# Masking and storing the sorted attention weights block by block in steps 3 to 6 of a recurrent scan, and loading the sorted rows of steps 8 to 11 in step 4

## The chip, the cores and the metric

The kernel runs on one core of one Trainium2 chip, in one launch. The metric is the device time in microseconds (us) of a run; of the kernel before there are three such runs, and one more execution that was profiled. Everything below that carries a start time is taken from that profiled execution, counted from the start of its span.

## What is computed

A batch of 1024 users, each with a history of 100 item embeddings of 128 numbers, goes through two recurrent scans. Cut to what matters here:

```python
keys = GRU(history)                                  # [1024, 100, 128]
score = MLP(concat(keys, q, keys - q, q * keys))     # q: the item in question
attn = softmax(where(mask == 1, score, -inf))        # over the 100 steps
pooled = einsum('bt,btd->bd', attn, keys)            # [1024, 128]
att_seq = pooled.T[:100]        # column t of pooled is the weight of step t
def augru_step(h, (x_t, a_t)):                       # x_t = keys[:, t]
    r = sigmoid([h, x_t] @ Wr.T + br)
    u = sigmoid([h, x_t] @ Wu.T + bu)
    h_hat = tanh([h * r, x_t] @ Wh.T + bh)
    u = a_t[:, None] * u
    return (1 - u) * h + u * h_hat
attention_feature = state of the step sequential_length - 1
scores = MLP(concat(user, item, hist_sum, item * hist_sum, attention_feature))
```

The update weight `a_t` of the second scan (AUGRU) is a column of `pooled`: it is known only when the whole first scan, the softmax and the pooled sum are done.

## The kernel before, in words

The batch lies along the free dimension: a tile is 128 hidden units by 512 users, and there are two halves (`i` = 0 and 1). The first part, `gru_phase`, runs the 100 steps of the GRU with the attention scores, the running softmax and the pooled sum beside them. It ends at about 1400 us of the span.

The second part, `augru_phase`, runs steps 1 to 99 of AUGRU on users sorted by length, so that a column is dropped when its user's history is over. Three versions of it are in the program (for three shapes of the list of lengths), and a branch picks one; the one that ran here starts with 384 columns per half and has 44 at the end. The constants give for it: `one` = 88, `cover[99]` = columns 340 to 384, and `LAST * PR` = 320.

Steps 1 to 87 run as half steps, `half_step(t, i)`, each with six matrix products of 384 columns at first. In one half step TensorE (PE) does: the product of the half before with `r` (`ph`, line 1425), the products with this half's state (`pr`, `pu`, line 1425), and the three products with the keys of the half after (`open_gates`, line 1421). VectorE (DVE) does, in this order: `pu*c` of the half before (1465), `r = h*pr` (1467), the new state of the half before (1469), `pu*att` (1470), `rest` (1473), and the transposition of the keys of step t+2 (`load_key`, 1403). ScalarE (ACT) does three activations. The two halves alternate, so PE fills the time in which one half waits for its activations. Steps 88 to 99 do both halves at once (`whole_step`); there a single chain through PE, ACT and DVE sets the pace.

What surrounds the change:

- **The weights.** `store_pooled` (1296) writes `pooled` to HBM in 8 stores. `gather_weights` (indirect DMAs by POOL, line 195) reads the users back in sorted order, four gathers for each half, into `att_r`. `mask_weights` (1358) zeroes the weights behind each user's end, in one DVE operation over the steps 4 to 99. `store_weights` turns the result in four blocks of 32 steps (transpositions, 1364) and stores each to `late_d` (1368); `load_att` (1387) then reads the row of one step back, spread over 128 partitions, into `at`. The rows of step 4 are read behind the first block's store, those of step t+2 in step t from step 3 on. Steps 1 to 3 have their weights from another, earlier path (`att_d`).
- **The queues.** All these stores and loads but the gathers are issued by SyncE (SP), in program order; a load that waits for a store to land holds whatever SP issues behind it.
- **The sorted rows.** The keys of steps 0 to 11 lie in HBM sorted by user (`sorted_d`). Those of steps 8 to 11 are loaded by `load_sorted` (242) into two tiles of the pool `kp3`; the first transposition from them is `load_key(8, i)` in step 6. The keys of step 12 on come by row gathers (POOL, 249), each behind a one-column copy (248) that paces it by `rest`.
- **The predictor.** The last MLP runs for groups of 128 users when their columns are over. For three groups it is a generator, `predict_held`, that `whole_step` advances three times in a step: `turn()` between the openings of `pr`/`pu` and the closing of `ph`, `turn()` between the opening of `ph` and the products with `rest`, and once at the end of the step. The row product is `rows` (1638); for the second and third group the last product of the group before (1637) stands ahead of it.

Of the kernel before, what the change touches and what calls it, by code (L numbers as in the profile page):

```python
# [19 lines left out]
P = 128  # L20
B = 1024
T = 100
# [29 lines left out]
G = 4  # L52
# [61 lines left out]
def kernel(ctx: ExitStack, tc: tile.TileContext, a: dict, out: bass.AP):  # L114
# [123 lines left out]

    def load_sorted(q, i, tile):

        rows[q, i] = tile
        nc.sync.dma_start(out=tile[:, :, : G * R], in_=sorted_d[i][ts(q, P)])

# [1056 lines left out]
    def augru_phase(pools, alive, delay):  # L1300
# [17 lines left out]
        ]  # L1318
        one = apart[-1] + 1
        ends = group_ends(alive, delay)  # L1320
# [34 lines left out]

        def mask_weights(i):
            later_rows = sorted_rows[i][:, :, SOON:T]
            nc.vector.tensor_mul(later_rows, later_rows, used_s[:, i])

        def store_weights(i):  # L1360

            turned = wp.tile([P, P // R, GH * R], F32, tag="att_t", name="att_t", bufs=2)
            for b in range(P // R):
                nc.vector.transpose(
                    turned[:, b, :].rearrange("p (g r) -> p g r", r=R),
                    sorted_rows[i][:, :, ts(b, R)],
                )
                nc.sync.dma_start(
                    out=late_d[i][ts(b, R), :].rearrange("c (p s) -> p c s", s=P),
                    in_=turned[:, b, :],  # L1370
                )
                if b == 0:
                    load_att(SOON, i)

        def load_att(t, i):
# [60 lines left out]
        def half_step(t, i):  # L1436
# [40 lines left out]
            resets[t, i] = r, pu, rest  # L1477
            if (t, i) in ((2, 1), (3, 0)):
                mask_weights(t % 2)
            if (t, i) == (1, 0):  # L1480
# [3 lines left out]
            elif after[0] == one < T:  # L1484
                open_both(one, "pr", "pu", "ph")
            if (t, i) == (2, 1):
                store_weights(0)
            elif (t, i) == (3, 0):
                store_weights(1)
            if SOON - 2 < t < T - 2:  # L1490
# [102 lines left out]
        def predict_held(groups):  # L1593
# [19 lines left out]

            def state_of(g):
                state = sp.tile([P, NH, PR], F32, name="state3")
                nc.scalar.copy(state, h_all[:, :, ts(g, PR)])
                return state
# [15 lines left out]
            for k, g in enumerate(groups):  # L1633
                p = tile_of("rows")
                p2 = p[:, HB - 1 :]
                if k:
                    nc.tensor.matmul(p2, lhsT=f1, rhs=later["m2"], start=True, stop=True)
                nc.tensor.matmul(
                    p[:, :M0],
# [4 lines left out]
                )  # L1644
                yield
                yield
# [216 lines left out]
        sorted_rows = [gather_weights(i) for i in range(NH)]  # L1863
        for half in later["halves"]:
            load_sorted(2, half.i, kp.tile([P, KH, 2 * G * R], F32, tag="rows", name="rows"))
        ahead, due = iter(()), []
# [10 lines left out]
        for t in range(1, T):  # L1877
# [6 lines left out]
            for i in range(NH):  # L1884
                if t < one:
                    half_step(t, i)
                elif i == 0:
                    whole_step(t, lambda: next(held, None))
                for _ in range(due.pop(0) if due else 0):
                    next(ahead, None)  # L1890

                if t < one:
                    take_turn(2 * G)
                elif i == 0:
                    next(held, None)
# [10 lines left out]
            if t == HALF_TIME:  # L1906
                last_places()
                for m, to in zip((wr, wu), minus):
                    nc.gpsimd.tensor_scalar_mul(to, m[:, 0, :], -1.0)
                nc.gpsimd.tensor_scalar_mul(later["m0_minus"], later["m0"][:, 4, :], -1.0)  # L1910
        all_of(held)
        for _, job in jobs:
            all_of(job)
        earlier_results()
        if one == T:
            open_state(T - 1, 1)
            next(final)
            last_state(1)
        all_of(final)
# [102 lines left out]
```

## Time and profile before

| | us |
|---|---|
| median of 3 runs | 1978.48 (1976.69 to 1979.32) |
| the profiled execution's own time | 1971.09 |
| its span | 1968.9 |
| PE busy | 1957.7 of the span |
| DVE, ACT, POOL busy | 1637.3, 935.1, 1256.5 |
| bytes moved by DMA | 220.17 MB |

A row of the timeline gives the start, the length, the engine, the line, the operation with output and inputs, how many instructions are merged in the row, and in brackets the idle time before it with what ended it. Starts of consecutive rows of one line tell the pace: they can be closer than the lengths, since an engine starts one instruction while the last results of the one before are still coming out. Rows of SP are the issuing of a DMA and not its transfer.

### The profile page before, as it was taken

Reading aid. Unit: us, or ns where it says so; the run is one execution under the profiler, and the core shown is the slowest. Engines: PE = TensorE matmul, PEld = TensorE weight load, DVE = VectorE, ACT = ScalarE, POOL = GpSimd, SP = SyncE. Lnnn points to the kernel's source line nnn. Section 1 sums busy time; section 2 is a strip of 40 time slices with the busy share of each in tenths; the row PEclk is TensorE's granted clock in tenths of the full one; section 3 lists DMA queues with packets and bytes.
Section 4 is the critical chain, followed back from the end, with each engine's and each line's share of the span. In section 5 each row is a group of like instructions: output and inputs, shape, how many; then the busy total and the mean of one; then the engine's idle time right before and its main releaser. Section 6 shows DMA issues by size and latency. Waiting matters only on the chain.

```text
span 1968.9 us, 40928 instructions
## 1 busy us (share of the span) xinstructions
PE 1957.7 (99%) x15270; PEld 846.7 (43%) x15270; DVE 1637.3 (83%) x2976; ACT 935.1 (47%) x1676; POOL 1256.5 (64%) x1348
## 2 busy tenths in 40 slices
PE   9999999999999999999999999999999999999998
PEld 3333333333333333333333333333555556789898
DVE  7888888888888888888878888888787788888896
ACT  4444454454545454454545444455444444455554
POOL 1324859678696969688695949798754444454432
PEclk9999999999999999999999999999999999999999
DMA  4453333233333443347743333323543333335441
GB/s 117 110 110 103 109 100 102 77 99 117 107 112 116 102 119 102 91 139 218 208 157 109 99 104 108 94 81 122 156 140 103 98 98 94 103 93 120 115 81 40
DMA packets 257173, 220.17 MB, mean 112 GB/s; under 512 B 53871, under 2 KB 219348, under 8 KB 256196
## 3 DMA queue, kind: packets, MB, share of 16 engines
q1 hardware_dynamic: 245476, 185.15, 33.7%
q0 software_dynamic: 11200, 32.04, 5.6%
q8 instruction: 122, 2.00, 0.4%
q14 instruction: 87, 0.71, 0.1%
q10 hardware_dynamic: 288, 0.26, 0.0%
HBM read 154.90 MB, written 60.85 MB: 110 GB/s over the span
## 4 chain that ended last, share of the span: by engine, by line
PE 97%; POOL 1%; DMA 1%; DVE 0%; SPq 0%; issue 0%; ACT 0%; another core or an unknown queue 0%; POOLq 0%; DVEq 0%; ACTq 0%
PE ps L665 52%; PE pm L851 17%; PE ph L1425 4%; PE pu L1425 4%; PE pr L1425 4%; PE pu L1421 4%; PE ph L1421 4%; PE pr L1421 4%; POOL pooled L777 1%; POOL kw L776 1%; PE pr L1516 0%; DMA x<-in_hist_x 0%; DMA att_r<-pooled_d,idx_w 0%; PE pu L1516 0%; PE ph L1516 0%
## 5 line engine op out<-in xcount | busy, mean ns | idle before, releaser
L665 PE MATMUL ps<-x,wih 128*32 128x512 f32 (+1 forms) x4808 | 588.1, 591 | 1.7 <-DMA x<-in_hist_x 1.4
L665 PE MATMUL ps<-hn,whh 128*32 128x512 f32 x4752 | 582.7, 592 | 0.0
L677 ACT ACTIVATE r<-ps,brz 128x512 f32<-128x512 f32 x200 | 137.8, 689 | 446.2 <-PE ps L665 443.4
L665 PEld LDWEIGHTS ps<-x,wih 128*32 128x32 f32 x4808 | 157.6, 110 | 359.5 <-issue 319.6
L665 PEld LDWEIGHTS ps<-hn,whh 128*32 128x32 f32 x4752 | 155.7, 110 | 354.1 <-issue 350.8
L649 POOL TENSOR_TENSOR xm<-x,m 128x512 f32<-128x512 f32 x200 | 234.3, 1172 | 74.3 <-DMA m<-mask_d 73.7
L650 POOL TENSOR_TENSOR hist<-hist,xm 128x512 f32<-128x512 f32 x200 | 258.8, 1294 | 15.7
L777 POOL TENSOR_TENSOR pooled<-pooled,kw 128x512 f32<-128x512 f32 (+1 forms) x195 | 250.2, 1283 | 15.3
L776 POOL TENSOR_TENSOR kw<-kt,e 128x512 f32<-128x512 f32 (+1 forms) x195 | 210.0, 1077 | 70.4 <-DVE e L1009 70.4
L249 POOL DMA_INDIRECT rows<-keys_d,idx_k x186 | 180.4, 970 | 75.8 <-POOL rows L248 69.3
L685 DVE SCALAR_TENSOR_TENSOR u<-ps,bhh,r 128x512 f32<-128x512 f32 x198 | 147.8, 747 | 91.3 <-PE ps L665 88.4
L698 ACT ACTIVATE ps<-ps,bih 128x512 f32<-128x512 f32 x198 | 131.1, 662 | 189.0 <-DVE ps L695 189.0
L1433 ACT ACTIVATE c<-ph,bh 128x384 f32<-128x384 f32 (+38 forms) x174 | 88.2, 507 | 257.0 <-PE ph L1425 256.9
L851 PE MATMUL pm<-hn,wk 128*32 128x512 f32 x1188 | 205.8, 592 | 0.0
L851 PE MATMUL pm<-kq,wkq 128*32 128x512 f32 x1188 | 205.7, 592 | 0.0
L851 PE MATMUL pm<-mv,w 128*32 128x512 f32 x790 | 187.6, 592 | 0.0
L708 DVE TENSOR_TENSOR d<-hn,ps 128x512 f32<-128x512 f32 x198 | 136.1, 688 | 36.0 <-ACT ps L698 35.9
L248 POOL COPY rows<-rest 128x1 f32<-128x1 f32 x186 | 35.4, 190 | 196.8 <-DVE rest L1473 176.2
L709 DVE TENSOR_TENSOR d<-ps,d 128x512 f32<-128x512 f32 x198 | 137.0, 692 | 26.4 <-ACT ps L699 14.3
L695 DVE TENSOR_TENSOR ps<-ps,u 128x512 f32<-128x512 f32 x200 | 139.9, 700 | 22.6 <-PE ps L665 1.9
L710 DVE TENSOR_TENSOR ps<-ps,d 128x512 f32<-128x512 f32 x198 | 138.4, 699 | 6.7
L730 DVE STREAM_TRANSPOSE kt<-hn 128x512 f32<-128x512 f32 x200 | 140.3, 701 | 3.3 <-ACT hn L717 3.3
(342 smaller groups left out, 3000.3 us busy)
## 6 DMA issues: line engine op xcount, KB each, us to landing
x<-in_hist_x SPq DMA_DIRECT2D x211, 256.0 KB
keys_d<-kt SPq DMA_DIRECT2D x44, 1024.0 KB
m<-mask_d SPq DMA_DIRECT2D x200, 128.0 KB
at<-late_d SPq DMA_DIRECT2D x46, 192.0 KB
wide_d<-kt SPq DMA_DIRECT2D x24, 256.0 KB
sorted_d<-sort SPq DMA_DIRECT2D x32, 192.0 KB
rows<-sorted_d SPq DMA_DIRECT2D x6, 1024.0 KB
s_b<-mv SPq DMA_DIRECT2D x200, 8.0 KB
```

Of the source, the lines that this page charges most:

```text
L249: nc.gpsimd.indirect_dma_start(out=r[:, k, :], out_offset=None, in_=keys_d[q], in_offset=bass.IndirectOffsetOnAxis(ap=idx_k[:, k, i : i + ...
L649: nc.gpsimd.tensor_mul(d, x, m)
L650: nc.gpsimd.tensor_add(acc, acc, d)
L665: nc.tensor.matmul(p[ts(q, R), cs], lhsT=w[:, g, ts(q, R)], rhs=v[:, cs], start=(j == 0), stop=(j == len(parts) - 1),)
L685: nc.vector.scalar_tensor_tensor(out=u, in0=ph, scalar=bhh[:, 2:3], in1=r, op0=ALU.add, op1=ALU.mult,)
L695: nc.vector.tensor_add(pi, pi, u)
L730: nc.vector.transpose(kt[:, :, n, :], h.rearrange("p (k r) -> p k r", r=R))
L776: eng.tensor_mul(d, k, w)
L777: eng.tensor_add(acc, acc, d)
L851: nc.tensor.matmul(p[i][s, :], lhsT=w[:, s], rhs=v, start=start, stop=stop)
L1421: nc.tensor.matmul(p, lhsT=m[:, 1, :], rhs=v, start=True, stop=False)
L1425: nc.tensor.matmul(p, lhsT=m[:, 0, :], rhs=v, start=False, stop=True)
```

## The change

The one DVE operation that masked a half's weights is cut into four, one for each block of 32 steps, and `store_weights` becomes a generator: a half step of the steps 3 to 6 takes one block, masks it, turns it, stores it, and (first block) loads the row of step 4. Before, half 0 was masked, turned and stored whole in half step (2, 1), and half 1 in (3, 0). The load of the sorted rows of steps 8 to 11 moves from the start of AUGRU to behind the half steps of step 4, and takes the 12 blocks of users that are in use instead of 16. In `predict_held` one `yield` moves up, so that the row product comes a turn later. The new formula for `one` gives 88 again for the version that ran; the branch at the end of `augru_phase` is for `one == T`, which that version does not reach; the assertion makes no instruction.

```diff
-    def load_sorted(q, i, tile):
+    def load_sorted(q, i, tile, n=KH):
         rows[q, i] = tile
-        nc.sync.dma_start(out=tile[:, :, : G * R], in_=sorted_d[i][ts(q, P)])
+        nc.sync.dma_start(out=tile[:, :n, : G * R], in_=sorted_d[i][ts(q, P), :n])
...
-        one = apart[-1] + 1
+        one = T if cover[T - 1][0] < LAST * PR else apart[-1] + 1
...
-        def mask_weights(i):
-            later_rows = sorted_rows[i][:, :, SOON:T]
-            nc.vector.tensor_mul(later_rows, later_rows, used_s[:, i])
-
         def store_weights(i):
             turned = wp.tile([P, P // R, GH * R], F32, tag="att_t", name="att_t", bufs=2)
             for b in range(P // R):
+                steps = slice(max(SOON, b * R), min(T, (b + 1) * R))
+                later_rows = sorted_rows[i][:, :, steps]
+                nc.vector.tensor_mul(
+                    later_rows,
+                    later_rows,
+                    used_s[:, i, :, steps.start - SOON : steps.stop - SOON],
+                )
                 nc.vector.transpose(
...
                 if b == 0:
                     load_att(SOON, i)
+                yield
...
-            if (t, i) in ((2, 1), (3, 0)):
-                mask_weights(t % 2)
             if (t, i) == (1, 0):
                 open_gates(1, 1, ("pr", "pu"))
...
-            if (t, i) == (2, 1):
-                store_weights(0)
-            elif (t, i) == (3, 0):
-                store_weights(1)
+            if t == G - 1:
+                stores.append(store_weights(i))
+            if t >= G - 1 and stores:
+                next(stores[i], None)
             if SOON - 2 < t < T - 2:
                 load_att(t + 2, i)
...
                 if k:
                     nc.tensor.matmul(p2, lhsT=f1, rhs=later["m2"], start=True, stop=True)
+                yield
                 nc.tensor.matmul(
                     p[:, :M0],
...
-                yield
                 yield
                 if k:
                     result(groups[k - 1], p2)
...
-        for half in later["halves"]:
-            load_sorted(2, half.i, kp.tile([P, KH, 2 * G * R], F32, tag="rows", name="rows"))
+        stores = []
+        third = [kp.tile([P, KH, 2 * G * R], F32, tag="rows", name="rows") for _ in range(NH)]
...
                     half_step(t, i)
+                    if t == G:
+                        load_sorted(2, i, third[i], blocks[FIRST[2]].stop)
```

On DVE, from the last `rest` of half step (2, 1) on, the program before reads (numbers behind a name tell buffers apart; `att_r` are the gathered weights, `att_t` the turned ones, `k` the keys, `c` the tanh):

```order
L1473 SCALAR_TENSOR_TENSOR rest<-pu,h_all 128x384
L1358 TENSOR_TENSOR att_r<-att_r,used_s 128x4x96
L1364 STREAM_TRANSPOSE att_t<-att_r 128x128 x4
L1403 STREAM_TRANSPOSE k_14904<-rows 128x384
L1465 TENSOR_TENSOR pu<-pu,c_14907 128x384
L1467 TENSOR_TENSOR r_14914<-h_all,pr 128x384
L1469 TENSOR_TENSOR h_all<-pu,rest 128x384
L1470 TENSOR_TENSOR pu<-pu,at 128x384
```

Half step (3, 0) begins at `pu<-pu,c`. In the same place the changed program has on DVE:

```order
L1477 SCALAR_TENSOR_TENSOR rest<-pu,h_all 128x384
L1407 STREAM_TRANSPOSE k_14890<-rows 128x384
L1469 TENSOR_TENSOR pu<-pu,c_14893 128x384
L1471 TENSOR_TENSOR r_14900<-h_all,pr 128x384
L1473 TENSOR_TENSOR h_all<-pu,rest 128x384
L1474 TENSOR_TENSOR pu<-pu,at 128x384
L1477 SCALAR_TENSOR_TENSOR rest<-pu,h_all 128x384
L1362 TENSOR_TENSOR att_r<-att_r,used_s 128x4x28
L1367 STREAM_TRANSPOSE att_t<-att_r 128x128
```

The mask of half 0 now stands one half step (six DVE operations) later, and one block of it at a time. On SP, the program before issues at the start of AUGRU (`late_d_82` is that of half 0, `late_d_83` of half 1):

```order
L1296 DMA pooled_d<-pooled 32x16x32 x8
L242 DMA rows<-sorted_d_72 128x16x128
L242 DMA rows<-sorted_d_73 128x16x128
L1368 DMA late_d_82<-att_t 4x32x128
L1387 DMA at<-late_d_82 128x384
L1368 DMA late_d_82<-att_t 4x32x128 x3
L1368 DMA late_d_83<-att_t 4x32x128
L1387 DMA at<-late_d_83 128x384
L1368 DMA late_d_83<-att_t 4x32x128 x3
```

The changed program issues there, on SP:

```order
L1296 DMA pooled_d<-pooled 32x16x32 x8
L1371 DMA late_d_82<-att_t 4x32x128
L1391 DMA at<-late_d_82 128x384 x2
L1371 DMA late_d_83<-att_t 4x32x128
L1391 DMA at<-late_d_83 128x384 x2
L1371 DMA late_d_82<-att_t 4x32x128
L1391 DMA at<-late_d_82 128x384
L242 DMA rows<-sorted_d_72 128x12x128
L1371 DMA late_d_83<-att_t 4x32x128
L1391 DMA at<-late_d_83 128x384
L242 DMA rows<-sorted_d_73 128x12x128
```

The loads of the sorted rows went behind the first store of each half and its loads; the second load of `at` behind each first store is that of step 5. On PE, the third group's row product in the whole steps of the program before (`m_9352` are the weights of the attention feature):

```order
L1506 MATMUL pu<-k_19765,wu 128x88
L1637 MATMUL rows<-m_9646,f_19785 128x1
L1638 MATMUL rows<-m_9352,state_19787 128x200
L1516 MATMUL ph<-r_19803,wh 128x88
L1506 MATMUL ph<-k_19765,wh 128x88
L1516 MATMUL pr<-rest,minus_14754 128x88
```

and in the changed program on PE:

```order
L1508 MATMUL pu<-k_19771,wu 128x88
L1640 MATMUL rows<-m_9646,f_19791 128x1
L1518 MATMUL ph<-r_19808,wh 128x88
L1508 MATMUL ph<-k_19771,wh 128x88
L1642 MATMUL rows<-m_9352,state_19793 128x200
L1518 MATMUL pr<-rest,minus_14754 128x88
```

The product of 200 columns moved from ahead of the closing of `ph` to behind its opening.

More of the change, by code (lines that the diff above doesn't have):

```diff
@@ L1614, in state_of @@
             def state_of(g):
+                assert ends[g] < t
                 state = sp.tile([P, NH, PR], F32, name="state3")
@@ L1910, in augru_phase @@
                 nc.gpsimd.tensor_scalar_mul(later["m0_minus"], later["m0"][:, 4, :], -1.0)
+        if one == T:
+            open_state(T - 1, 1)
+            last_state(1)
         all_of(held)
@@ L1914, in augru_phase @@
         earlier_results()
[L1915 to L1918, printed above, removed]
         all_of(final)
```

## The prediction

> **What bounds the kernel now.** I read the page first, for the engine that sets the end, then PE's and DVE's waits, then the timeline where the longest of them falls.
>
> ```profile
> span 1968.9 us, 40928 instructions
> PE 1957.7 (99%) x15270; PEld 846.7 (43%) x15270; DVE 1637.3 (83%) x2976; ACT 935.1 (47%) x1676; POOL 1256.5 (64%) x1348
> PE ph L1425 <- DVE r L1467: 2.9, 2, 2.8
> DVE att_r L1358 <- DMA att_r<-pooled_d,idx_w: 3.6, 1, 3.6
> ```
>
> PE is busy 99% of the span, so only what PE loses can be won: 1968.9 - 1957.7 = 11.2 us are not busy, and the change adds and removes no matrix product. Its one long wait is 2.8 us for `r` from DVE, and DVE's one wait of that size is 3.6 us for the gathered weights, ahead of the mask. PE's closings of `ph` show the place:
>
> ```profile
> 1418.10 0.81 PE L1425 MATMUL ph<-r,wh 128*128 128x384 f32 x2
> 1424.88 0.91 PE L1425 MATMUL ph<-r,wh 128*128 128x384 f32 x2 [2.75 <-DVE r L1467]
> 1429.17 0.91 PE L1425 MATMUL ph<-r,wh 128*128 128x384 f32 x2 [0.15 <-DVE r L1467]
> 1433.15 0.81 PE L1425 MATMUL ph<-r,wh 128*128 128x384 f32 x2
> 1437.02 0.81 PE L1425 MATMUL ph<-r,wh 128*128 128x384 f32 x2
> ```
>
> The last two are one half step apart: 3.87 us. Three half steps lie between 1418.10 and 1433.15, which is 15.05 us where 3 x 3.87 = 11.61 would do. PE loses **3.44 us** here, more than the idle times of 2.75 and 0.15, because the second and third closings come late too. DVE over the same stretch:
>
> ```profile
> 1415.69 0.57 DVE L1465 TENSOR_TENSOR pu<-pu,c 128x384 f32<-128x384 f32 x1 [0.78 <-ACT c L1433]
> 1416.31 0.55 DVE L1467 TENSOR_TENSOR r<-h_all,pr 128x384 f32<-128x384 f32 x1
> 1417.25 0.56 DVE L1470 TENSOR_TENSOR pu<-pu,s_b 128x384 f32<-128x384 f32 x1
> 1417.84 0.56 DVE L1473 SCALAR_TENSOR_TENSOR rest<-pu,h_all 128x384 f32<-128x384 f32 x1
> 1421.98 0.56 DVE L1358 TENSOR_TENSOR att_r<-att_r,used_s 128x384 f32<-128x384 f32 x1 [3.59 <-DMA att_r<-pooled_d,idx_w]
> 1422.58 0.89 DVE L1364 STREAM_TRANSPOSE att_t<-att_r 128x128 f32<-128x128 f32 x4
> 1432.44 0.56 DVE L1470 TENSOR_TENSOR pu<-pu,at 128x384 f32<-128x384 f32 x1
> 1435.23 0.56 DVE L1467 TENSOR_TENSOR r<-h_all,pr 128x384 f32<-128x384 f32 x1
> 1438.48 0.57 DVE L1465 TENSOR_TENSOR pu<-pu,c 128x384 f32<-128x384 f32 x1 [0.61 <-ACT c L1433]
> 1938.53 0.30 DVE L1565 TENSOR_TENSOR pu<-pu,at 128x128 f32<-128x128 f32 x1
> ```
>
> Behind the mask at 1421.98 stand in DVE's queue the four turns and half step (3, 0) with its `r`, which PE waits for. Two margins matter for later. In a settled half step DVE idles 0.61 us (1438.48). And `r` is done at 1435.23 + 0.56 = 1435.79, while PE takes it at 1437.02: **1.23 us** by which DVE may be late before PE loses anything.
>
> **Part 1: the mask moves one half step on.** I put the half steps on PE's undisturbed pace. `r` of (2, 1) at 1416.31 served the closing at 1418.10. Then `r` comes at 1420.18 for (3, 0), 1424.05 for (3, 1), 1427.92 for (4, 0), 1431.79 for (4, 1). `rest` begins 1.53 us after `r` (1417.84 - 1416.31) and is over some 0.5 later, so DVE reaches the first mask of half 0 at about 1422.2 and that of half 1 at about 1426.1. When are the weights there?
>
> ```profile
> 1417.03 0.94 POOL L195 DMA_INDIRECT att_r<-pooled_d,idx_w  x1 [0.31 <-issue]
> 1422.03 1.33 POOL L195 DMA_INDIRECT att_r<-pooled_d,idx_w  x1 [0.30 <-issue]
> DMA to landing us min/median/max: 3.7/5.2/5.9
> 1411.54 2.63 SPq L242 DMA_DIRECT2D rows<-sorted_d  x2
> 1415.00:1420.00 5.00, 5.00 (x17) 2.92 (x16) 2.62 (x5) 2.62 (x5) 3.78 (x5) 1.00 0.94 343
> 1420.00:1425.00 5.00, 2.25 (x8) 1.07 (x7) 2.98 (x9) 0.76 (x2) 2.75 (x3) 1.00 0.22 66
> ```
>
> These are the last gather of each half, the time from issue to landing of all eight, the issue of the two sorted loads, and two windows (last columns: granted clock, DMA share, GB/s). The last gather of half 0 landed by 1421.98, 4.95 us after its issue; the mask at 1422.2 finds it there. The last gather of half 1 is issued at 1422.03 in either kernel, since POOL's issuing of eight in a row sets that; with 4.95 it lands at 1427.0, 0.9 us behind DVE. So the wait of 3.59 goes, and 0.9 us of waiting (none with 3.7, 1.8 with 5.9) may come one half step later, which the 1.23 us of margin cover, but for the longest landing. Nothing in it costs PE by itself, so this part is worth **-3.44 us**. The two sorted loads also leave the time of the gathers: 1415 to 1420 is when the rings were 0.94 busy. That can only shorten the landings; I count nothing for it, for the issuing of half 1's last gather does not move.
>
> **Part 2: the cut mask.** One operation of 384 elements becomes three of about 128 and one of 16 per half, a block each half step from (3, 0) to (6, 1). A DVE product of 128 elements takes 0.30 us (1938.53), a turn 0.89 / 4 = 0.22. That is 0.52 us more per half step against 0.61 of idle: nothing on PE's path, and were the idle time gone, at most 8 x 0.52 = 4.2 us against the 1.23 of margin; but it stands there in the row. The Trainium skill's page "VectorE: DVE Perf Modes", section "The DRAIN you can't avoid", speaks against cutting an operation: the next one does not start until the pipe is empty, so one should minimize the count. By that, the six operations of a half step would fill six times their length, 6 x 0.56 = 3.36, and mask and turn 0.57 more, together 3.93 us and 0.06 more than PE's 3.87; over six half steps 0.4 us, still inside the margin. The trace has starts closer than lengths: from `r` at 1435.23 to the idle time that ends at 1438.48, five operations pass in 3.25 - 0.61 = 2.64 us, 0.53 each for a length of 0.56. So I keep the 0.52.
>
> **Part 3: the rows of step 4 come back later, relative to their use.** This is what is late next. Before, store and load had slack, because PE had lost 3.44 us; now the store is issued at the same moment and its user is earlier.
>
> ```profile
> 1422.91 0.57 SPq L1368 DMA_DIRECT2D late_d<-att_t  x1
> 1425.52 0.34 SPq L1387 DMA_DIRECT2D at<-late_d  x1
> 1425.95 2.40 SPq L1368 DMA_DIRECT2D late_d<-att_t  x4
> 1431.79 0.34 SPq L1387 DMA_DIRECT2D at<-late_d  x1
> ```
>
> Half 0: mask and turn from 1422.2 to about 1422.8, store, and the load 2.61 us later as here (1425.52 - 1422.91), at 1425.4. How long a load of `at` takes to land, no row says. It is no less than the store's 2.61 (three times the bytes), and no more than the 4.4 us that the second one had: its user stands one half step behind 1432.44, at 1436.2, and shows no wait. So it lands between 1428.0 and 1429.8. (4, 0) needs it 0.94 us after its `r` (1417.25 - 1416.31), at 1428.9: 0 to 0.9 us of waiting, inside the margin of 1.23. Half 1: masked when its gather has landed, 1427.0, stored at 1427.6. In the row of four stores the fourth is half 1's first, issued about 1427.8, and the load that waits for it went out at 1431.79, 4.0 us later, among other transfers. With 2.6 to 4.0 the load goes out at 1430.2 to 1431.6 and lands at 1432.8 to 1436.0. Its user is due at 1431.79 + 0.94 = 1432.7, and PE loses from 1432.7 + 1.23 = 1434.0 on. The middle of the landings, 1434.4, costs 0.4 us; the ends cost nothing and 2.0. I take **+0.2**, toward the low end, since fewer stores are under way than in that row. What SP holds meanwhile: behind the waiting load stand the `at` of step 5, due a whole step later, and the second block's store, whose steps 32 on nobody reads before step 30. The DMA page of the Trainium skill, "DMA: Bandwidth & Descriptors", section "Anatomy of one DMA", gives 2.0 us plus the bytes over 436 GB/s; by it an estimate for the load (196,608 bytes) is 2.45 us, and with that for both loads this part would cost 0 and the time be 0.2 lower. The store of 65,536 bytes would be 2.15 us by the same rule, and the row has 2.61.
>
> **Part 4: the sorted rows of steps 8 to 11.** 12 of 16 blocks: 786,432 bytes a half. They go out after the second block's store, about 1431 to 1433 for half 0 and 1435 to 1437 for half 1. `load_key(8, 0)` stands 2.7 us behind `pu*c` of (6, 0): 1419.56 + 6 x 3.87 + 2.7 = 1445.5, and half 1's at 1449.3. Two such loads of 1 MB ran in the window of 343 GB/s; at that rate one takes 2.3 us, and even doubled, with 2 us of latency, half 1 is in at about 1444. Nothing, unless the rate collapses (rival below). The row gathers of POOL start some 3 us earlier than before and share the rings; they are due in step 10.
>
> **Part 5: the predictor's row product.** In the whole steps PE, ACT and DVE wait for each other in turn, so the place of a product counts.
>
> ```profile
> 1948.05 0.25 DVE L1564 TENSOR_TENSOR r<-h_all,pr 128x88 f32<-128x88 f32 x1 [0.45 <-ACT pr L1553]
> 1948.36 0.58 PE L1638 MATMUL rows<-m,state 128*128 128x200 f32 x2
> 1948.78 0.35 PE L1516 MATMUL ph<-r,wh 128*128 128x88 f32 x2
> 1949.41 0.39 PE L1516 MATMUL pu<-rest,minus 128*128 128x88 f32 x2
> 1949.84 0.46 PE L1516 MATMUL pr<-c,wr 128*128 128x88 f32 x2
> 1950.67 0.25 DVE L1564 TENSOR_TENSOR r<-h_all,pr 128x88 f32<-128x88 f32 x1 [0.30 <-ACT pr L1553]
> 1950.97 0.46 PE L1516 MATMUL ph<-r,wh 128*128 128x88 f32 x2
> ```
>
> Without the product `ph` begins 0.30 us behind the start of `r` (1950.97 - 1950.67); with it 0.73. So its 0.42 us (1948.78 - 1948.36) lie on the chain. Behind the opening of `ph` they fall where PE has room: the last product with `rest` is done at about 1949.63 and `pr<-c` starts at 1949.84, 0.2 us of the 0.42. I expect 0.42 won and 0.22 given back, **-0.2** for each of the second and third group, and nothing for the first, which has no product ahead of it: -0.4 in all. Bounds: everything won, 2 x 0.42 = -0.84; or all of it put back behind `ph`, 0.
>
> **The sum.** -3.44 + 0.2 - 0.4 = -3.64 us. The profiled execution would go from 1971.09 to 1967.45. The three runs lie 5.6 to 8.2 us above that execution, for a reason the page doesn't show; the gain is a count of microseconds at one place, so I take it off their median: 1978.48 - 3.64 = **1974.8**.
>
> **Rivals.** *The read-back becomes the wait.* The landings of gathers, store and load all come out at their long ends, and `at` of (4, 1) costs 2.0 us, with half 0 waiting ahead of it. For: no slack is left there, and the four transfers in a row are all of the kind whose landings spread from 3.7 to 5.9. Against: the rings are 0.22 busy in 1420 to 1425. Gain 3.44 - 2.0 and perhaps 0.4: 1.4 to 1.8, so 1976.7 to 1977.1. *The sorted rows come too late, and it gets slower.* Place: the key turns of step 6, which PE follows one to one. Half 1's load must land by 1449.3 + 1.23 = 1450.5. Both halves are 1.57 MB from 1432 on, so it decides below 1.57 MB / 18.5 us = 85 GB/s. At the 66 GB/s of the emptier window above they take 23.8 us, 5.3 too many: 1980.1, slower than before; the loss eats the whole gain below 71 GB/s, and 0.2% more below 60. Against: 343 GB/s was reached with the same kind of load. *The change doesn't remove the stall*: the weights land later still, and half step (3, 0) waits as (2, 1) did: 1978.5. Against: the last gather's issue hangs on POOL alone.
>
> **How the numbers follow.** About 0.2% (3.96 us) is what a measurement of this kernel can tell from no change: faster means below 1974.5, slower above 1982.4. My forecast stands 0.3 us from the first line, so it is split. Stall gone, little comes instead: 0.77, true values 1974.2 (full end gain, no read-back cost) to 1975.8, and runs that scatter as the three did, 1.8 us below their median to 0.8 above; 0.36 of it below the line, 0.41 above. Read-back rival 0.13, all within 0.2%. Sorted rows 0.07, of which 0.05 slower and 0.02 within. Stall stays 0.03, within. Faster 0.36, same 0.59, slower 0.05. The range goes from 1974.2 less 1.8 to 1977.1 and 0.8 for scatter: 1972.4 to 1977.9.
>
> **What would show it.** Right: DVE's first mask at about 1422 without a wait, the second with under 1 us; closings of `ph` 3.87 us apart from 1418 to 1441; PE's wait for `r` gone from its list; `ph` 0.3 us behind `r` in every whole step. Wrong: a DVE wait on `pu<-pu,at` of steps 4 or 5 followed by PE idle, a wait of a key turn for `rows<-sorted_d` at 1445 to 1455, or closings of `ph` still 4 us apart while the masks are cut.

## The result and the profile after

| | changed | before, same chip | ratio (95%) |
|---|---|---|---|
| first timing | 1974.20 us (1970.99 to 1977.64, 22 runs) | 1976.97 us (1974.14 to 1980.75, 22 runs) | 0.9984 (0.9978 to 0.9989) |
| again, another chip (`e8_after`) | 1973.47 us (1971.29 to 1976.94, 9 runs) | 1978.09 us (1974.90 to 1981.23, 19 runs) | 0.9975 (0.9965 to 0.9985) |

The first ratio is 3.2 us less (2.2 to 4.3), the second 4.9 us less (3.0 to 6.9); 3.64 were forecast. The time lies 0.6 us from the forecast 1974.8, and the gain just inside the 0.2% that were called no change.

The profiled execution of the changed kernel does not show a gain at all. Its page:

```profile
span 1969.8 us, 40932 instructions
PE 1959.3 (99%) x15270; PEld 846.4 (43%) x15270; DVE 1637.6 (83%) x2982; ACT 934.9 (47%) x1676; POOL 1256.4 (64%) x1348
```

The span is 0.9 us *longer* than the 1968.9 of the kernel before. So I went to the place itself. PE's closings of `ph` in the changed kernel's timeline:

```profile
1417.69 0.81 PE L1429 MATMUL ph<-r,wh 128*128 128x384 f32 x2
1421.56 0.81 PE L1429 MATMUL ph<-r,wh 128*128 128x384 f32 x2
1425.43 0.81 PE L1429 MATMUL ph<-r,wh 128*128 128x384 f32 x2
1429.30 0.81 PE L1429 MATMUL ph<-r,wh 128*128 128x384 f32 x2
1433.17 0.81 PE L1429 MATMUL ph<-r,wh 128*128 128x384 f32 x2
```

They are 3.87 us apart throughout: the 3.44 us are gone here. DVE in the same timeline, with the two first masks and the only wait for a transfer:

```profile
1421.83 0.27 DVE L1362 TENSOR_TENSOR att_r<-att_r,used_s 128x112 f32<-128x112 f32 x1
1426.58 0.26 DVE L1362 TENSOR_TENSOR att_r<-att_r,used_s 128x112 f32<-128x112 f32 x1
1433.22 0.57 DVE L1474 TENSOR_TENSOR pu<-pu,at 128x384 f32<-128x384 f32 x1 [0.58 <-DMA at<-late_d]
```

Neither mask has a bracket, so neither waits; `at` of (4, 1) waits 0.58 us, and the closing behind it at 1437.04 does not feel it. The span must then have been lost elsewhere. ScalarE's (ACT's) rows of the changed kernel at two places:

```profile
1424.91 0.56 ACT L1464 ACTIVATE pu<-pu,bu 128x384 f32<-128x384 f32 x1 [1.31 <-PE pr L1425]
1427.10 0.58 ACT L1437 ACTIVATE c<-ph,bh 128x384 f32<-128x384 f32 x1 [1.63 <-PE pr L1429]
...
1824.74 0.43 ACT L1437 ACTIVATE c<-ph,bh 128x198 f32<-128x198 f32 x1 [2.45 <-PE ph L1425]
```

`c` at 1824.74 needs the closing of `ph`, a row that ends at 1823.10, and ACT itself is free from 1822.29 on; it starts 1.64 us after both. I call that a **late start**: the start, less the later of the end of the closing and the end of ACT's own operation before. In settled half steps it is under 0.1 us. This profile has eight of over 0.5 us, among them 1.25 and 0.86 at the two rows ahead of the dots; the first profile of before has none in all of AUGRU. The late ones at steps 62 to 86 cost 5.2 us, which hides the gain in the span. Whether they belong to the change had to be settled first, and what each part of the change is worth without them.

To read the place in every kernel alike, I use one length: from the start of `r` of (2, 1) to that of (7, 1) on DVE. These are ten half steps, 38.70 us at 3.87 each. In before it is 42.14, in the changed kernel 38.70.

### The profile page after: what moved, and what is told of

Same layout as the page of the kernel before. It is cut to its first block, busy times and chain, and to the rows that moved or that the text cites. A ratio compares the mean times of both kernels' runs of the same rounds, so it can differ in the third digit from the quotient of the medians.

```text
span 1969.8 us, 40932 instructions
## 1 busy us (share of the span) xinstructions
PE 1959.3 (99%) x15270; PEld 846.4 (43%) x15270; DVE 1637.6 (83%) x2982; ACT 934.9 (47%) x1676; POOL 1256.4 (64%) x1348
## 4 chain that ended last, share of the span: by engine, by line
PE 98%; DMA 1%; DVE 1%; issue 0%; ACT 0%; SPq 0%; DVEq 0%; ACTq 0%
PE ps L665 52%; PE pm L851 17%; PE ph L1429 4%; PE pu L1425 4%; PE ph L1425 4%; PE pr L1425 4%; PE pu L1429 4%; PE pr L1429 4%; PE last L819 1%; DMA x<-in_hist_x 0%; PE pr L1518 0%; DMA at<-late_d 0%; PE pu L1518 0%; PE ph L1518 0%; PE last L851 0%
```

## The experiments

Twelve runs were made, on four chips, and the kernel before was timed on each: `e1` to `e4`, `e5` to `e8`, `e9` to `e11`, and `e12` share a chip. "Length" is the one just defined, "late" the late starts of over 0.5 us within it.

| kernel | length | wait of the masks | late | ratio to before (95%) |
|---|---|---|---|---|
| before, first profile | 42.14 | 3.59 | none | |
| changed, first profile | 38.70 | 0 | 1.25, 0.86 | 0.9984 (0.9978 to 0.9989) |
| `e1_sorted` | 40.53 | 1.20, 0.69 | none | 0.9994 (0.9985 to 1.0002) |
| `e2_blocks` | 41.03 | 0 | 2.65, 0.85 | 0.9993 (0.9984 to 1.0001) |
| `e3_product` | 41.71 | 3.15 | none | 0.9998 (0.9989 to 1.0006) |
| `e4_shift` | 41.49 | 0 | 2.84, 1.02 | 1.0007 (0.9998 to 1.0016) |
| `e5_before` | 41.84 | 3.29 | none | one run |
| `e6_whole` | 40.64 | 0 | 2.93 | 0.9990 (0.9981 to 1.0000) |
| `e7_pads` | 40.20 | 0.51 | 2.26 | one run |
| `e8_after` | 42.69 | 0 | 0.72, 3.81 | 0.9975 (0.9965 to 0.9985) |
| `e9_later` | 38.71 | 0 | none | 0.9982 (0.9973 to 0.9991) |
| `e10_all` | 38.70 | 0 | none | 0.9984 (0.9975 to 0.9993) |
| `e11_after` | 38.70 | 0 | none | one run |
| `e12_blocks` | 40.40 | 0 | 1.90, 0.82, 0.93 | 0.9981 (0.9972 to 0.9990) |

**`e1_sorted`: only the sorted loads move.**

```diff
-        for half in later["halves"]:
-            load_sorted(2, half.i, kp.tile([P, KH, 2 * G * R], F32, tag="rows", name="rows"))
...
                     half_step(t, i)
+                    if t == G:
+                        load_sorted(2, i, third[i], blocks[FIRST[2]].stop)
```

> The kernel before with only the sorted rows of steps 8 to 11 loaded in step 4, in 12 blocks. Theory 'place' (the loss comes from where the mask stands in DVE's queue, and the landing of the gathered weights is set by POOL's issuing): the mask in half step (2, 1) still waits 2.4 us or more, up to 3.6, and PE loses 2.2 to 3.4 us there; ratio 0.999 to 1.000. Rival 'contention' (the sorted loads in the rings made the gathers late): the last gather of half 0 lands 3.7 us or less after its issue instead of 4.95, and PE's loss falls to 2.2 us or less. Late starts with nothing shown that they waited for, of which the changed kernel's profile has 5 us between steps 62 and 86: if they are chance, they fall in other steps here or not at all; if they belong to the change, they are absent here.

The last gather of half 0, POOL's row in this kernel, and both masks on DVE:

```profile
1417.36 0.94 POOL L195 DMA_INDIRECT att_r<-pooled_d,idx_w  x1 [0.30 <-issue]
```

```profile
1419.89 0.56 DVE L1358 TENSOR_TENSOR att_r<-att_r,used_s 128x384 f32<-128x384 f32 x1 [1.20 <-DMA att_r<-pooled_d,idx_w]
1424.97 0.56 DVE L1358 TENSOR_TENSOR att_r<-att_r,used_s 128x384 f32<-128x384 f32 x1 [0.69 <-DMA att_r<-pooled_d,idx_w]
```

From issue to landing it takes 2.53 us (1419.89 - 1417.36), where it was 4.95 beside the sorted loads; DMA is 0.19 busy from 1415 to 1420 instead of 0.94. The changed kernel, which moves the loads too, has the same short landings; over the weight gathers of `e9_later` (the changed kernel with a later edit that leaves them alone) the view shows, where that of before had 3.7/5.2/5.9:

```profile
DMA to landing us min/median/max: 2.4/2.5/2.6
```

So 'contention' held: POOL's issuing alone does not set the landing, the traffic beside it does as much. The unmoved masks wait 1.89 us together instead of 3.59, and the length falls by 1.61. Late starts come in this kernel as well, so they don't need the masks' move.

**`e2_blocks` and `e12_blocks`: only the masks and stores, block by block; the sorted loads stay.** One kernel, run on two chips.

```diff
-            if (t, i) in ((2, 1), (3, 0)):
-                mask_weights(t % 2)
...
+            if t == G - 1:
+                stores.append(store_weights(i))
+            if t >= G - 1 and stores:
+                next(stores[i], None)
```

> The kernel before with only the masks and stores block by block in steps 3 to 6, the sorted rows still loaded at the start. 'Place': the first mask waits 0 to 0.3 us, PE's closings of ph stay 3.87 us apart, the loss of 3.44 us falls to 0.5 or less, ratio 0.9983 plus or minus 0.0008. 'Contention': the gathers land late beside the sorted loads, the first and second mask wait over 1 us, and 1 us or more of PE's loss remains. Late starts without a cause: elsewhere than in steps 62, 77 and 85 if chance, there again if they belong to the block-wise store.

> The masks and stores block by block with the sorted loads left at the start, again, in the hope of a chip on which no activation starts late: the chip of the last three runs had none in the whole scan, the two chips before it had them in every kernel, among them an activation 2.65 us late at 1425 in this very kernel. Theory 'move of the masks alone': if no activation comes late here, the masks do not wait over 0.6 us, closings of ph stay 3.87 us apart, the transition gives all of its 3.4 us, and the time is 2.5 to 4 us below before; the moved sorted loads then add nothing to the change. Rival 'both are needed': without a late activation a mask still waits over 1.2 us for the gathers beside the sorted loads, and the gain is 1 to 2 us. If activations start late here as well, the run tells nothing new of this.

The masks do not wait in either run, with the DMA engines 0.94 and 0.88 busy from 1415 to 1420. But the length falls by only 1.11 and 1.74 us, short of what 'place' had expected, and what is lost stands behind ACT. `e2_blocks`, PE and then ACT:

```profile
1417.88 0.81 PE L1429 MATMUL ph<-r,wh 128*128 128x384 f32 x2
1421.75 0.81 PE L1429 MATMUL ph<-r,wh 128*128 128x384 f32 x2
1427.83 0.91 PE L1429 MATMUL ph<-r,wh 128*128 128x384 f32 x2 [1.07 <-DVE r L1471]
```

```profile
1425.21 0.58 ACT L1437 ACTIVATE c<-ph,bh 128x384 f32<-128x384 f32 x1 [4.59 <-PE ph L1425]
1426.64 0.56 ACT L1462 ACTIVATE pr<-pr,br 128x384 f32<-128x384 f32 x1 [0.84 <-PE ph L1425]
```

The closing at 1421.75 is over at 1422.56; its `c` starts 2.65 us later, with ACT free since 1420.63. `pr` behind it is late by 0.85, so DVE's `r` is, so PE is. The "4.59" of the bracket is ACT's whole idle time and says nothing of the cause: 2 us of it are usual in a half step. The first mask's loss is gone before any late start: the closings for half steps (2, 1) and (3, 0) are 3.87 us apart (1421.75 - 1417.88; in `e12_blocks`, `e4_shift` and `e7_pads` too), where before has 6.78. No mask waits, so "both are needed" does not hold as a matter of gathers; but both chips had late starts, and how much the masks' move alone gains in the whole scan without them stays open. In the timed runs it is 1.4 us (-0.2 to 3.2) on the one chip and 3.8 (2.0 to 5.5) on the other.

**`e3_product`: only the predictor's row product.**

```diff
                     nc.tensor.matmul(p2, lhsT=f1, rhs=later["m2"], start=True, stop=True)
+                yield
...
-                yield
                 yield
```

> The kernel before with only the predictor's row product one turn later. If the gain at the end is the product's: the eleven whole steps from the first closing of ph (step 88) to the last (step 99) take 26.4 us instead of 26.8, PE's loss of 3.44 us at the mask stays, ratio 0.9998. Rival, the difference of 0.4 us between the two profiles is chance: 26.8 plus or minus 0.15.

The place of the masks is as before (3.15 us of waiting). From `r` of step 88 to that of step 99 it takes 1943.37 to 1969.85, DVE's rows: 26.48 us. Before has 26.98, the kernels without this part 27.05 to 27.16, those with it 26.48 to 26.53. So the product's move is worth 0.5 us, as expected from the profile, and below what the timed runs can tell (0.9998).

**`e4_shift` and `e6_whole`: mask and store left whole, half a step later;** in `e6_whole` the sorted loads move too.

```diff
-            if (t, i) in ((2, 1), (3, 0)):
-                mask_weights(t % 2)
+            if t == G - 1:
+                mask_weights(i)
...
-            if (t, i) == (2, 1):
-                store_weights(0)
-            elif (t, i) == (3, 0):
-                store_weights(1)
+            if t == G - 1:
+                store_weights(i)
```

> The kernel before with mask and store of each half whole, but one half step later (half 0 in (3, 0), half 1 in (3, 1)), nothing cut. 'Place' (moving it behind the landing is what counts): DVE has 1.45 us more in each of the two half steps, against 0.61 of idle and 1.23 of margin; PE loses 0 to 0.6 us instead of 3.44, ratio 0.9983 to 0.9986. Rival 'cut' (the cutting into blocks is needed): the four turns in a row make r late by more than the margin, twice, and 1.5 us or more of PE's loss remain, ratio 0.999 or more.

> The mask and the store stay whole and stand one half step later, and the sorted loads go to step 4: the change without the cut and without the product's move. If moving alone wins (theory 'both moves, no cut'): neither mask waits; mask and turns take 1.45 us in one half step, against 0.61 of idle plus 1.23 of margin, so PE's closings lose at most 0.5 us per half, a gain at the transition of 2.5 to 3.45 us and a time 2 to 3.5 us below before. If ScalarE's late start at the first masks comes whatever the rings do (rival 'late start stays'): an activation starts 2 to 3 us late at 1425 as in the shift without the move of the loads, and the gain is under 1 us. If the cut is needed (rival 'cut'): the read-back of step 4 comes 1 us later behind the turns, and the product with it waits over 1.2 us.

No mask waits in either. Both have a late start in half step (3, 1); ACT and DVE's `r` behind it in `e4_shift`, then ACT in `e6_whole`:

```profile
1426.16 0.56 ACT L1458 ACTIVATE pr<-pr,br 128x384 f32<-128x384 f32 x1 [2.87 <-issue]
1427.74 0.56 ACT L1460 ACTIVATE pu<-pu,bu 128x384 f32<-128x384 f32 x1 [1.02 <-remote]
1426.75 0.55 DVE L1467 TENSOR_TENSOR r<-h_all,pr 128x384 f32<-128x384 f32 x1 [2.22 <-issue]
```

```profile
1426.76 0.56 ACT L1460 ACTIVATE pu<-pu,bu 128x384 f32<-128x384 f32 x1 [2.98 <-PE ph L1425]
```

In `e4_shift` the numbers are those of rival 'cut': 2.79 us of the loss remain (41.49 - 38.70), and the ratio is 1.0007. But its mechanism is not shown: DVE has been through the four turns and idle for 2.22 us when `r` starts behind ACT's late `pr`. In `e6_whole`, with the sorted loads out of the way, the late start is 2.93 us all the same, so they are not what makes it. `e6_whole` gains 1.50 us of length, between the two expectations, and is 2.0 us faster (0 to 3.8). Its `at` of (4, 1) waits 1.04 us, under the 1.2 of rival 'cut'. Whether the cut is worth anything can't be told under late starts of that size.

**`e5_before`: the kernel before, a second profile.** No edit.

> The kernel before, unchanged, profiled a second time. In the first profile of it no activation of AUGRU starts more than 0.5 us after both its input and ScalarE are there; in the five other profiles seven to ten activations do, at the same numbers in ScalarE's list (320, 388, 391, 480, 527 from the branch on), for 0.6 to 2.8 us each. If these late starts belong to the program (theory 'everywhere'), this profile has them too, the mask wait of 3.1 to 3.6 us and PE's loss of 3.4 us at the first masks stay, and the end of the scan is 6 to 9 us later than in the first profile of before. If they belong to something that all the changed kernels share (theory 'changed'), this profile is like the first, within 1 us.

'Everywhere' held, with 5.8 us at the end just under the 6 expected. The place of the masks is as in the first profile (3.29 us of waiting, length 41.84), and of the five late starts this is the first, a closing on PE and its `c` on ACT:

```profile
1825.92 0.50 PE L1425 MATMUL ph<-r,wh 128*128 128x198 f32 x2
```

```profile
1828.03 0.43 ACT L1433 ACTIVATE c<-ph,bh 128x198 f32<-128x198 f32 x1 [2.43 <-PE ph L1421]
1828.74 0.40 ACT L1458 ACTIVATE pr<-pr,br 128x192 f32<-128x192 f32 x1 [0.28 <-PE ph L1421]
```

From 1826.42 to 1828.03, 1.61 us, at the same activation as in the changed kernel at 1824.74. Its `r` of step 99 comes 5.8 us later than in the first profile, and so does its time, 1976.91 against 1971.09. So the late starts are not of the change; the first profile of before is the one without.

**`e7_pads`: `e2_blocks` with twelve activations that feed nothing.**

```diff
             nc.scalar.activation(u, pu, AF.Sigmoid, bias=later["bu"])
+            if (t, i) in ((1, 0), (1, 1), (2, 0)):
+                for _ in range(4):
+                    nc.scalar.activation(pad, later["br"], AF.Sigmoid)
```

> Block by block masks with the sorted loads at the start, and 12 extra activations of one column on ScalarE, four in each of the half steps (1,0), (1,1) and (2,0), where it idles 2 us and more; they feed nothing. Without them the late starts stand at activations 15 and 16 (2.65 and 0.85 us) and at 388, 391 and 527. If they hang on ScalarE's place in its instruction list (theory 'address'), they stay at these numbers counted with the extra ones, which is four half steps earlier in the scan: at 1407 to 1411 instead of 1425, before the sorted loads are even issued, and 8 us earlier around 1820; then the half step at the first masks is free and PE's closings there 3.9 us apart. If they hang on what the kernel does there (theory 'traffic': the loads on the rings), they stay in the same half steps, numbers 27, 28, 400, 403 and 539, at 1425 and 1828, with sizes as before.

ACT at the masks in this kernel:

```profile
1425.71 0.56 ACT L1463 ACTIVATE pr<-pr,br 128x384 f32<-128x384 f32 x1 [2.26 <-PE pu L1426]
```

The late start stays in half step (3, 1), at number 28 instead of 15 and 16, and the later ones at the same half steps around 1825, 1901 and 1925, with other sizes. So it does not hang on ACT's place in its instruction list; 'address' fell. 'Traffic' is what is left of the two, but by `e6_whole` the sorted loads are not that traffic.

**`e8_after` and `e11_after`: the changed kernel, two more profiles.** No edit.

> The changed kernel again, on this chip. Time against before 0.9978 to 0.9989 as first measured, so 2 to 4 us less. In the profile: no mask wait, closings of ph through the first masks 3.87 us apart, late activations again at numbers 388, 391, 480 and 527 (theory 'everywhere'), and at 17 and 18 with 1.3 us or less. If the late starts fall on chance, numbers and sizes differ from the first profile of it.

> The changed kernel a third time, one profile. By what its two profiles show, the masks do not wait, and the late start at activations 17 and 18 has a size between 0.7 and 3.8 us; with under 1.3 us the closings of ph lose at most 0.3 us from 1418 to 1436, with more they lose the excess over 1.23 us of margin. If the late start were of the change, its size would be alike in the three profiles.

In `e8_after` the late starts take more than the whole gain. ACT's rows:

```profile
1424.59 0.56 ACT L1464 ACTIVATE pu<-pu,bu 128x384 f32<-128x384 f32 x1 [0.77 <-PE pr L1425]
1430.26 0.58 ACT L1437 ACTIVATE c<-ph,bh 128x384 f32<-128x384 f32 x1 [5.11 <-PE ph L1425]
```

`c` at 1430.26 is 3.81 us late, where at most 1.3 had been expected, and PE stands. PE's next row, and the window from 1430 to 1435, whose 0.66 is the granted clock (the share of TensorE's full clock that the profile shows as granted):

```profile
1430.89 1.08 PE L1425 MATMUL pu<-k,wu 128*128 128x384 f32 x2 [1.86 <-ACT c L1437]
1430.00:1435.00 5.00, 4.11 (x7) 2.11 (x8) 3.94 (x9) 2.17 (x5) 1.00 (x2) 0.66 0.32 105
```

In the first profile of before PE stood for 2.75 us, and the clock stayed at 1.00; so the length of the stop alone does not tell when it falls. The length here is 42.69, more than the 42.14 of before. This execution, 1976.94 us, is the slowest of the nine of this run, of which the fastest took 1971.29. `e11_after` fell on a chip without late starts, which none of its expectations had foreseen, and shows the change plainly. Its page:

```profile
span 1965.3 us, 40932 instructions
PE 1958.1 (100%) x15270; PEld 1130.4 (58%) x15270; DVE 1638.7 (83%) x2982; ACT 934.5 (48%) x1676; POOL 1256.5 (64%) x1348
```

PE loses 7.2 us in the whole span (1965.3 - 1958.1), where it lost 11.2. On the same chip the kernel before took 1970.29 us (1969.13 to 1972.67, 21 runs), in which its first profile (1971.09) fits, while its medians on the other chips are 1976.97 to 1980.95. It is the same program; the chip differs, and the hour, and no run separates the two. In the profiles with late starts `r` loses 4.8 to 11.1 us against the first profile of before between steps 50 and 88, where the three on this chip lose less than 0.2.

**`e9_later` and `e10_all`: the row gathers begin later.** `e9_later` delays those for steps 12 to 19 by four half steps; `e10_all` the later groups by one step as well.

```diff
-            return spread_over(n, NH * (FIRST[q] - t + 1 - early))
+            wait = 4 if q == WIDE else 0
+            return [0] * wait + spread_over(n, NH * (FIRST[q] - t + 1 - early) - wait)
```

> The changed kernel with the row gathers for steps 12 to 19 begun in step 5 instead of step 3, four half steps later and closer together. In all profiles with free masks so far an activation of half step (3,1) or (4,0) starts 0.7 to 3.8 us late near 1424 to 1430, with or without the sorted loads, just when POOL goes from the weight gathers to the row gathers and the rings carry at and rows together. Theory 'row gathers': without them there no activation starts over 0.5 us late between 1418 and 1436, and closings of ph stay 3.87 us apart; what comes late then comes at 1431 to 1440, and the time is 0 to 3 us below the changed kernel's. Rival 'whatever is loaded': an activation is still 0.7 to 3.8 us late at 1424 to 1430. The gathers are due in step 10; if they come too late, a key turn of step 10 waits for rows and the time is above that of the changed kernel.

> As the run before, and every later group of row gathers begins one step later too. The late activations at numbers 388 and 391 (1824 to 1833) stand where POOL issues row gathers without a pause beside a load of sorted rows, those at 480 and 527 beside the gathers for the predictor. Theory 'row gathers': these late starts move by one step or shrink to under half of 0.8 to 1.7 us each, and the time falls by up to 3 us more. Rival 'place': they stay at the same numbers with the same sizes and the time is that of the run before within 2 us.

They ran on the chip of `e11_after`, where the changed kernel without this edit has no late start either, so they can't tell what makes one; their times are that of `e11_after` within 0.5 us. They tell something else. SP's rows of the read-back of half 1, first in `e11_after` and then in `e9_later`:

```profile
1427.05 0.55 SPq L1371 DMA_DIRECT2D late_d<-att_t  x1
1430.86 0.80 SPq L1391 DMA_DIRECT2D at<-late_d  x2
```

```profile
1426.91 0.55 SPq L1371 DMA_DIRECT2D late_d<-att_t  x1
1429.49 0.80 SPq L1391 DMA_DIRECT2D at<-late_d  x2
```

The load goes out when the store has landed: 3.81 us with the row gathers beside it (DMA 0.55 busy from 1425 to 1430), 2.58 without (0.29). It is tempting to put the difference down to the gathers, but the first profile of the changed kernel has them too, and DMA 0.58 busy, and there the same store took 2.71 us:

```profile
1427.21 0.55 SPq L1371 DMA_DIRECT2D late_d<-att_t  x1
1429.92 0.80 SPq L1391 DMA_DIRECT2D at<-late_d  x2
```

In `e9_later` `at` of (4, 1) is not waited for at all. PE gains nothing by that, for it had not lost anything: lengths 38.70 and 38.71, and the ratios of the two kernels are those of the change.

## Why the prediction was right

**Part 1, the mask half a step on: -3.44 forecast, -3.44 measured** (length 42.14 to 38.70, in four profiles of kernels with this part, three of them without a late start). Within it one step was wrong: "I count nothing" for the sorted loads, because POOL's issuing sets the landings. By `e1_sorted` the loads made up half of the landing, 2.4 of 4.95 us, and moving them alone gains 1.61 us of length. It did not matter for the sum, since the masks stand late enough for either landing: they wait nothing beside the sorted loads (`e2_blocks`, `e4_shift`, `e12_blocks`) but once 0.51 us (`e7_pads`). The second mask's 0.9 us of waiting did not come.

**Part 2, the cut: 0 forecast, 0 measured.** DVE's rows of `e11_after`, for this and the next two parts:

```profile
1416.66 0.55 DVE L1471 TENSOR_TENSOR r<-h_all,pr 128x384 f32<-128x384 f32 x1
1419.91 0.57 DVE L1469 TENSOR_TENSOR pu<-pu,c 128x384 f32<-128x384 f32 x1 [0.68 <-ACT c L1437]
1427.65 0.57 DVE L1469 TENSOR_TENSOR pu<-pu,c 128x384 f32<-128x384 f32 x1 [0.17 <-ACT c L1437]
1434.39 0.57 DVE L1474 TENSOR_TENSOR pu<-pu,at 128x384 f32<-128x384 f32 x1 [1.23 <-DMA at<-late_d]
1455.36 0.55 DVE L1471 TENSOR_TENSOR r<-h_all,pr 128x384 f32<-128x384 f32 x1
...
1929.76 0.33 DVE L1566 TENSOR_TENSOR r<-h_all,pr 128x168 f32<-128x168 f32 x1 [0.40 <-ACT pr L1555]
1956.25 0.25 DVE L1566 TENSOR_TENSOR r<-h_all,pr 128x88 f32<-128x88 f32 x1 [0.61 <-ACT pr L1555]
```

A block takes 0.51 us of a half step's idle time (0.68 - 0.17), 0.52 were forecast. Since 0.17 us of idling is left, the trace does not agree with the rule that the prediction took from the Trainium skill's page "VectorE: DVE Perf Modes", section "The DRAIN you can't avoid", by which the half step would have been over-full. The same section adds that a next operation that is not held starts earlier, which the prediction left out and which fits these rows.

**Part 3, the read-back: +0.2 forecast, 0 measured.** This term was mis-sized by the 0.2 us, though what it says of the landing held. On the forecast's time scale (`r` of (2, 1) at 1416.31 there, at 1416.66 here, so 0.35 less) the load goes out at 1430.5 and `at` lands by 1434.04: inside the ranges 1430.2 to 1431.6 and 1432.8 to 1436.0. A cost of 0.2 stood for a landing at 1434.2, so by the forecast's own margin 0.04 was due. DVE waits 1.23 us, as much as the margin that I had counted, but part of that is idle time that it would have had anyway: `r` of (5, 0) comes 0.98 us behind the pace (1436.99, where 1432.14 + 3.87 = 1436.01), is over at 1437.53, and PE takes it at 1437.80. So 0.27 us of slack is left, and the closings stay 3.87 apart. The load took at most 3.53 us (1434.39 - 1430.86) with the DMA engines 0.56 busy. By the Trainium skill's page "DMA: Bandwidth & Descriptors", section "Anatomy of one DMA", an estimate is 2.45 us; the trace does not agree, and the page's fit is for DMAs that GpSimd issues, while SP issues this one. The first rival, a read-back that becomes the wait, stood close: a landing 0.3 us later would have cost PE time.

**Part 4, the sorted rows: 0 forecast, 0 measured.** No key turn waits for them in any profile. The slower rival needed under 85 GB/s; with the loads under way, from 1435 to 1440, `e11_after` moves 258 GB/s in all.

**Part 5, the product: -0.4 forecast, -0.5 measured** (1956.25 - 1929.76 = 26.49, before 26.98). PE in the changed kernel, the third group's step and the one ahead of it:

```profile
1947.18 0.41 PE L1518 MATMUL ph<-r,wh 128*128 128x88 f32 x2
1948.30 0.46 PE L1518 MATMUL pr<-c,wr 128*128 128x88 f32 x2
...
1949.44 0.45 PE L1518 MATMUL ph<-r,wh 128*128 128x88 f32 x2
1949.95 0.54 PE L1642 MATMUL rows<-m,state 128*128 128x200 f32 x2
1950.73 0.39 PE L1518 MATMUL pr<-c,wr 128*128 128x88 f32 x2
```

`ph` now begins 0.31 us behind its `r` (1949.13), where it was 0.73; from `ph` to `pr<-c` it takes 1.29 us with the product between and 1.12 without. So 0.42 is won and 0.17 given back, nearly as forecast (0.42 and 0.22).

**The sum and its base.** From the first `r` of AUGRU to the last, `e11_after` is 3.98 us shorter than the first profile of before (3.44, 0.49, and 0.05 over many places); its time is 1967.08 against 1971.09, 4.0 us less, and 3.2 less than the median of before on its own chip. The forecast took 3.64 off the median of three runs, which lay 5.6 to 8.2 us above the profile "for a reason the page doesn't show". The runs make the late starts the likely reason: that profile has none, and `e5_before`, with five, takes 5.8 us longer. That the time came out within 0.6 us is in part luck: the median of the three, 1978.48, lay 1.5 us above that of all 22 runs of before, 1976.97, and the two medians differ by 2.8 us instead of 3.64, so that two errors nearly cancel.

## What to carry to other kernels

A span is no measure of a change of three microseconds: measure from one operation to the same operation ten half steps later, in several profiles of both kernels. Moving the waiting operation behind work that must be done anyway took out its whole wait even where no transfer became faster (`e2_blocks`, `e12_blocks`, `e4_shift`), and making the transfer faster alone took out half (`e1_sorted`). What decides next is the following transfer in the chain, whose slack is what DVE may wait before PE does; here DVE waited 1.23 us, at no cost, and 0.27 us were left.

## What the runs showed of the hardware

**Activations that start late on some chips.** On three of the four chips of the experiments, and in the first profile of the changed kernel, ScalarE starts five to nine operations of AUGRU 0.5 to 3.8 us after both input and engine are there; on the fourth chip, in three kernels, there is none, and there the kernel before takes 1970.29 us instead of 1977.77 to 1980.95. They come in the same half steps in every kernel: near 1425, unless the masks hold PE up there, near 1824 to 1834, 1902 and 1925, and in some profiles between 1778 and 1815, with sizes that differ from execution to execution (0.72 and 3.81 us for neighbours in `e8_after`). They are not of the change (`e5_before`), nor of the sorted loads near 1425 (`e6_whole`), nor of ACT's place in its list (`e7_pads`). The Trainium skill's page "Runtime: NRT & Kernel Launch", section "Instruction fetch mechanics", has each engine's instructions come in blocks of 256. Up to the late start `e7_pads` has nine more instructions in ACT's list than `e2_blocks` (twelve activations more, three semaphore instructions fewer), and a settled half step has four; such a boundary would have moved by two half steps, and the late starts did not move. What makes them stays open: near 1425, 1826, 1902 and 1926 POOL issues indirect gathers one behind the other, but so it does from 1411 to 1422, where none is late, and the runs that moved the gathers fell on the chip without late starts.

**Landings beside other traffic.** The same gather landed 4.95 us after its issue beside two loads of 1 MB, and 2.53 us without them; on the chip of `e11_after`, without them, landings of such gathers are 2.4 to 2.7 us. For a 64 KB store the case is not made: it landed 2.71, 3.40 and 3.81 us after its issue in the three profiles of the changed kernel, with row gathers beside it, and 2.58 and 2.67 in the two kernels without, so the gathers may lengthen it, but do not always.
